# Two transformer layers with experts: expert numbers read once, stores on the queue of the engine that made them, and new ranks in the planner

## The chip, the cores and the metric

The kernel runs on one core of a Trainium2 chip, in one launch. The metric is the device time of one execution in microseconds (us). A core has five engines with an instruction queue each, worked off in order: TensorE (PE, matmuls and transposes), VectorE (DVE), ScalarE (ACT), GpSimd (POOL) and SyncE (SP), which computes nothing and issues DMAs. An instruction that waits holds up everything behind it in the queue of its engine. Semaphores tie the queues together.

## The reference

The input is 4,096 tokens of 128 numbers (16 sequences of 256). Two layers are applied; all is float32, and each half of a layer is followed by an addition and a layer norm:

```python
x = layernorm(x + attn0(rmsnorm(x)))   # 16 heads of 64, over the 256 tokens of a sequence
x = layernorm(x + shared(x) + experts0(x))   # best 2 of 8 experts, hidden 256, and a shared one
x = layernorm(x + attn1(x))            # a token's 16 heads of 8 attend to each other
x = layernorm(x + experts1(x))         # best 2 of 8 experts, hidden 512
```

An expert is GELU(x W1) W2, weighted by its softmax probability. The second attention is taken within each token: its scores are a 16 by 16 matrix per token.

## The kernel before

**Groups and waves.** Tokens are held in SBUF as eight groups of 512. Attention of layer 0 runs through the groups in units of two heads and one sequence: scores on TensorE (L574), row maxima on VectorE (L537), exponentials on ScalarE (L543), division by the sums on GpSimd (L558), transposes (L591) and the product with the values (L612) on TensorE. The expert halves run in waves over groups, `WAVES`: five waves in layer 0, three in layer 1 (the first holds groups 0 to 3, the second 4 and 5, the third 6 and half of 7). The other half of the last group goes through all experts densely (`sequence`, `dense`).

**One wave.** `route` computes on VectorE where each token goes (`r_pi`, L853) and which expert each tile of 128 rows has (`r_ei`, L867). `send` scatters the rows to DRAM on GpSimd, one indirect DMA per 128 tokens and choice (L905). `lists` then works through the tiles in fours, with these strands of its own:
- `loads_rows` loads four tiles of rows (L1014).
- `loads_first` loads per tile the weights of its expert. `expert_of` (L997) reads the expert's number from SBUF into a register of SyncE, and the DMA's address is worked out from that register. In layer 0 both weights come here (L1035, L1039), in layer 1 only the first one (L1039, 256 KB).
- `loads_second`, in layer 1 only, loads the second weight (L1048, 256 KB) into its own ring of buffers, and reads the expert's number again for it.
- `turns` transposes the rows (L1060), `firsts` multiplies by the first weights (L1098), `gelu` follows on ScalarE (L1071, L1077), `seconds` multiplies by the second weights (L1118).
- `stored` copies the result from PSUM into `yq` on VectorE or ScalarE (L270 or L272, in the helper `copied`) and stores four tiles to DRAM with one DMA (L1136), which SyncE issues.

When all tiles of a wave are stored, `gathered` fetches each token's two results on GpSimd (L934), and `normed` norms them: on VectorE (L399), or on ScalarE (L409) with two small GpSimd steps ahead. In layer 0 `attention1` follows for these tokens (L1216 to L1308), in layer 1 the output is stored (L1431 in `last`, L1595 in `sequence`) by SyncE. Only one wave at a time holds the buffers of `lists`.

**The order of the work.** Nothing of the order is left to a scheduler: the instructions are listed by a planner that runs while the kernel is built. Every strand is a generator that yields the time from which its next step can start and the engine it needs. `work` keeps a clock per engine from fixed costs, `moved` one for the DMA pipe. `everything` takes the strand with the best key: a time of favour and a rank from `KEYS` (for attention of layer 0 also `PACE`, one rank per half group), where a lower rank goes first among those that could start. `copied` gives a copy to the engine whose planned clock ends it first. So costs and ranks decide the listed order, the engine of a copy, and of a norm; what the chip then does can run ahead of or behind the plan, but each engine keeps its listed order.

```python
best = min(starts, key=lambda c: (max(c[0] - c[1].key[0], first), c[1].key[1:]))[1]
```

Of the kernel before, what the change touches and what calls it, by code (L numbers as in the profile page):

```python
# [28 lines left out]
LAST = NG - 1  # L29
# [8 lines left out]
def two_layers(  # L38
# [98 lines left out]
    def cleared(layer, w):  # L137
# [10 lines left out]

    INF = float("inf")
    KEYS = {  # L150
        "copy qk": (-0.126, 0.098),
        "copy v": (0.258, 0.464),
        "copy p": (0.365, 0.67),
        "copy o": (-2, 0.171),
        "softmax": (-0.332, 0.347),
        "softmax 2": (-0.557, 0.071),
        "summed": (-1.741, 0.444),
        "normalised": (0.126, 0.737),
        "heads": (-0.897, 0.036),
        "w route": (0.203, 0.017),  # L160
        "w send": (-0.299, 0.32),
        "w shared": (-0.925, 0.219),
        "w loads": (-0.335, 0.546),
        "w turns 0": (-0.74, 0.23),
        "w turns 1": (-0.883, 0.07),
        "w firsts 0": (-0.387, 0.019),
        "w firsts 1": (1.618, 0.545),
        "w gelu": (-0.526, 0.095),
        "w seconds 0": (-0.551, 0.301),
        "w seconds 1": (1.137, -0.645),  # L170
        "w stored": (-1.046, -0.735),
        "w gathered 0": (0.929, 0.295),
        "w gathered 1": (0.397, -0.379),
        "w qkv": (-1.874, 0.602),
        "w attention1": (0.552, 0.037),
        "w attention1 2": (0.862, 0.362),
        "w sums": (0.545, 0.099),
        "w normed": (-0.751, 0.178),
        "d loads": (-1.222, 0.561),
        "d route": (0.341, 0.516),  # L180
        "d firsts": (-0.612, -0.163),
        "d gelu": (0.532, 0.418),
        "d seconds": (-0.409, -0.744),
        "d added": (-0.448, 0.337),
        "d normed": (-0.4, 1.013),
    }
    PACE = [-1.37, 1.462, -1.273, -1.636, 1.503, -0.385, -0.54, 1.281]
    PACE += [1.979, 0.872, 0.936, -0.178, 0.47, 1.169, 0.679, 1.086]
    now = [0]
    COPY = -0.06  # L190
    SUMS = 7.789
    FAVOUR = 0.378
    SWITCH, SWITCH_BACK = 0.582, 1.515
    window, unit = [0, 0.0, 1.0], [P]
    clk = {"PE": 0.0, "DVE": 0.0, "ACT": 0.0, "POOL": 0.0, "SP": 0.0}
    table = ["exp"]
# [31 lines left out]
    def work(e, us, *after, ports=False, one=None, mode=P):  # L228

        at = max(clk[e], floor[0], *after)  # L230
        if ports and pool[0] - 0.15 > at:
            us += min(pool[0] - 0.15 - at, pool[1])
        clk[e] = (paced(at, us, mode) if e == "PE" else at + us) + SETUP[e]
        if one is not None:
            pool[:] = clk[e], one
        return clk[e] + 0.08

    def moved(size, *after, us=0.45, row=2048):

# [9 lines left out]
    def closed(place, at):  # L249
        ends[place[0]][place[1]] = at  # L250
        return at
# [129 lines left out]
        nc.gpsimd.tensor_tensor(r, v, mhalf[:, 0:n], ALU.pow)  # L381
        return r, work("POOL", 1.1, at)

    def normed(y, o, tag, at):
# [12 lines left out]
        if max(clk["DVE"], at) + 1.9 <= max(clk["ACT"], at) + 1.4:  # L397
            for c in range(n):
                nc.vector.tensor_scalar(  # L399
                    o[:, c, :], y[:, c, :], mv[:, c, 0:1], r[:, c : c + 1], ALU.subtract, ALU.mult  # L400
                )
            return work("DVE", 0.05 + 0.35 * n, at, ports=True)
# [7 lines left out]
        return work("ACT", 0.35 * n, at)  # L410

    def across(src, ring, at):

# [555 lines left out]
    def lists(r):  # L969
# [18 lines left out]
        starts = list(range(0, NT, QT))  # L988
        number = [min(NT, t0 + QT) - t0 for t0 in starts]
        N = len(starts)  # L990
        xqs, was, wbs, hs, xTs = {}, {}, {}, {}, {}
        gelued = {}
        downs = [0]
# [2 lines left out]
        def expert_of(t):  # L996
            return nc.values_load(  # L997
                r.expert[0:1, t : t + 1],
                engines=[mybir.EngineType.SP],
                min_val=0,  # L1000
                max_val=NE - 1,
                skip_runtime_bounds_check_because="the minimum with the last expert's number was taken",
            )
# [16 lines left out]
        def loads_first():  # L1020
            for i in range(N):
                if yields and i > 0 and urgent:
                    yield (lambda: INF if downs[0] < i else 0.0), None
                    held.remove("lists")
                    yield (lambda: INF if urgent or "lists" in held else 0.0), None
                    held.append("lists")
                for q in range(number[i]):

                    ring = WB if q % 2 and layer == 0 else WA
                    yield (lambda: max(r.listed, ring.free())), "SP"  # L1030
                    free = ring.free()
                    e = expert_of(starts[i] + q)
                    wa, k = ring.tile([P, 4, P], "wa")
                    if layer == 0:
                        nc.sync.dma_start(out=wa[:, 2:4], in_=second(e))  # L1035
# [3 lines left out]
                    nc.sync.dma_start(out=wa.rearrange("p c h -> p (c h)"), in_=w1[bass.ds(e * P, P), :])  # L1039
                    was[i, q] = wa, k, moved(131072 * (1 + layer), r.listed, free, us=0.45 + 0.4 * layer)  # L1040

        def loads_second():
            for i in range(N):
                for q in range(number[i]):
                    yield (lambda: INF if (i, q) not in was else WB.free()), "SP"
                    free = WB.free()
                    wb, k = WB.tile([P, 4, P], "wb")
                    nc.sync.dma_start(out=wb, in_=second(expert_of(starts[i] + q)))  # L1048
# [80 lines left out]
        def stored(i, place, po, at):  # L1129
            t0, n = starts[i], number[i]  # L1130
            yield (lambda: max(at, Y.free())), EITHER
            free = Y.free()
            y, k = Y.tile([P, QT, D], "yq")
            at = closed(place, copied(y[:, 0:n, :], po[:, 0:n, :], at, free))
            yield at, "SP"
            nc.sync.dma_start(  # L1136
                out=outs[layer][w][t0 * P : (t0 + n) * P, :].rearrange("(t p) d -> p t d", p=P),
                in_=y[:, 0:n, :],
            )
# [283 lines left out]
    def last(r, part):  # L1423
        g, c0, n = PARTS[part]
        at = yield from gathered(r, part, max(r.stored.values()))
        yield from taken("y1")
        y = sb.tile([P, n, D], FP, tag="y1", name="ye", bufs=1)
        at = yield from normed(tokens(part), y, "n1", at)
        yield at, "SP"
        b = c0 // 2  # L1430
        nc.sync.dma_start(  # L1431
            out=grouped(out, g)[:, b : b + n // 2], in_=y.rearrange("p (b c) d -> p b (c d)", b=n // 2)
        )
        held.remove("y1")
        return work("SP", 0.6, at)

    routed1 = []
    for i in range(len(WAVES[1])):
# [130 lines left out]
    def sequence(b=1):  # L1569
# [23 lines left out]
        at = yield from normed(x, y, "n1", at)  # L1593
        yield at, "SP"
        nc.sync.dma_start(out=grouped(out, LAST)[:, b], in_=y.rearrange("p c d -> p (c d)"))  # L1595
        held.remove("y1")
        work("SP", 0.6, at)

    begin(normalised(0), key("normalised"))
    begin(prepared(), key("normalised"))  # L1600
# [63 lines left out]
```

## Time and profile before

| what | us |
|---|---|
| median of 3 runs | 1215.32 (1213.84 to 1217.02) |
| the profiled execution, its own time | 1245.39 |
| its span, first to last instruction | 1243.7 |
| busy: TensorE (matmuls) | 1109.0 (89%) |
| busy: VectorE | 900.2 (72%) |
| busy: ScalarE | 706.0 (57%) |
| busy: GpSimd | 705.7 (57%) |
| granted TensorE clock, mean | 0.943 of full |
| DMA, mean over the span | 107 GB/s, 132.47 MB |

The profile shows one execution. Its times of single instructions, of stages and of waits add up to its own 1245.39 us and not to the median. A waiting line reads: engine and line, `<-` what ended the wait, then the sum of the waits in us, their number, the longest. A line of the timeline reads: start, length, engine, source line, operation, tiles, number; SPq is SyncE's queue of DMAs, and a merged line of several issues runs from the start of the first to the end of the last. A line of a source reads: operation, tiles, number, least/median/greatest duration in ns, first and last start.

### The profile page before, as it was taken

What the parts mean: (1) busy time and instruction counts of PE and PEld (TensorE: products, weight loads), DVE (VectorE), ACT (ScalarE), POOL (GpSimd) and SP (SyncE); (2) the same over time, 40 slices, a digit from 0 to 9 for tenths busy, and PEclk for the clock granted to TensorE, in tenths of its full rate; (3) what the DMA queues carried; (4) which work ended last, traced back from release to release, by engine and by line L of the source; (5) the groups of instructions that cost most, each with busy time, mean ns of one, the idle gap of its engine ahead of it and who ended that gap; (6) DMA issues with size and microseconds to landing.
All of it is one profiled execution on the core that took longest, in us unless ns stands there. A gap on an engine that the chain in (4) does not pass through costs nothing.

```text
span 1243.7 us, 22712 instructions
## 1 busy us (share of the span) xinstructions
PE 1109.0 (89%) x7336; PEld 814.5 (65%) x7336; DVE 900.2 (72%) x1811; ACT 706.0 (57%) x2050; POOL 705.7 (57%) x1089
## 2 busy tenths in 40 slices
PE   9999999979999999999998899987838896797883
PEld 5566667665665666766655677655738795697883
DVE  5767675478878888754877998888878795793433
ACT  5556566476665667676674687653544552342432
POOL 4434372557555468524769557767873546446666
PEclk9999999989999999999999999987888897798997
DMA  8900023430000021151003240135458874684952
GB/s 260 270 1 1 1 86 111 132 106 14 1 5 1 1 63 58 35 145 45 18 4 100 80 133 21 29 119 164 144 162 232 257 230 129 197 245 125 288 177 70
DMA packets 187208, 132.47 MB, mean 107 GB/s; under 512 B 12745, under 2 KB 171474, under 8 KB 187090
## 3 DMA queue, kind: packets, MB, share of 16 engines
q1 hardware_dynamic: 179410, 115.27, 31.6%
q0 software_dynamic: 7680, 15.74, 4.1%
q8 instruction: 59, 0.97, 0.3%
q14 instruction: 59, 0.48, 0.1%
HBM read 97.94 MB, written 33.03 MB: 105 GB/s over the span
## 4 chain that ended last, share of the span: by engine, by line
PE 66%; DVE 11%; POOL 8%; issue 6%; ACT 4%; DMA 2%; SPq 1%; ACTq 0%; DVEq 0%; POOLq 0%
PE s L574 9%; PE po L612 9%; PE t L591 9%; PE po_e L1118 6%; PE ph L1098 6%; POOL rows L905 5%; PE py L629 4%; PE pv L528 4%; PE pq L510 4%; PE pk L510 3%; DVE qk_prod L1216 2%; DMA xq<-rows 2%; PE po_d L1541 1%; POOL pr L558 1%; DVE sc L1220 1%
## 5 line engine op out<-in xcount | busy, mean ns | idle before, releaser
L558 POOL TENSOR_SCALAR pr<-pr,rs 128x256 f32<-128x256 f32 x512 | 253.0, 511 | 220.6 <-DVE rs L554 136.7
L543 ACT ACTIVATE pr<-s,nm 128x256 f32<-128x256 f32 x512 | 235.5, 474 | 26.1 <-DVE nm L537 23.0
L537 DVE TENSOR_REDUCE nm<-s 128x4 f32<-128x1024 f32 x128 | 156.1, 1220 | 58.0 <-PE s L574 53.2
L905 POOL DMA_INDIRECT rows<-x,r_pi x120 | 130.7, 1089 | 58.6 <-DVE r_pi L853 24.4
L934 POOL DMA_INDIRECT y<-outs,r_pi x120 | 120.0, 1000 | 65.8 <-issue 27.4
L612 PE MATMUL po<-pT,v 128*64 128x256 f32 x1024 | 146.0, 397 | 7.2 <-ACT h L1077 3.1
L1098 PE MATMUL ph<-xqT,wa 128*128 128x128 f32 x1028 | 132.8, 287 | 16.6 <-issue 14.2
L591 PE MATMUL t<-ident,pr 128*128 128x128 f32 x1024 | 144.4, 283 | 0.8 <-ACT h L1077 0.8
L591 PEld LDWEIGHTS t<-ident,pr 128*128 128x128 f32 x1024 | 115.7, 145 | 42.4 <-POOL pr L558 20.6
L1098 PEld LDWEIGHTS ph<-xqT,wa 128*128 128x128 f32 x1028 | 126.9, 202 | 22.6 <-issue 16.8
L270 DVE COPY pT<-t 128x512 f32<-128x512 f32 x163 | 106.8, 686 | 42.2 <-PE t L591 38.3
L574 PEld LDWEIGHTS s<-kT,qT 64*128 64x128 f32 x896 | 77.1, 186 | 84.2 <-issue 73.1
L574 PE MATMUL s<-kT,qT 64*128 64x256 f32 x896 | 127.0, 402 | 0.0
L1292 POOL TENSOR_TENSOR av_prod<-sc,qkv 128x1024 f32<-128x1024 f32 x35 | 89.9, 2577 | 50.7 <-ACT sc L1254 35.3
L272 ACT COPY oT<-po 128x256 f32<-128x256 f32 x99 | 36.9, 373 | 130.6 <-PE po L612 119.6
L612 PEld LDWEIGHTS po<-pT,v 128*64 128x64 f32 x1024 | 65.1, 137 | 67.6 <-issue 18.9
L543 ACT ACTIVATION_READ_ACCUMULATOR pr<-s,nm 128x1 f32 x512 | 105.5, 206 | 0.0
L1118 PE MATMUL po_e<-wb,h 128*128 128x128 f32 x648 | 84.3, 292 | 5.5 <-issue 5.5
L1118 PEld LDWEIGHTS po_e<-wb,h 128*128 128x128 f32 x648 | 82.6, 209 | 5.3 <-issue 4.8
L1216 DVE TENSOR_TENSOR qk_prod<-qkv 128x1024 f32<-128x1024 f32 x64 | 82.8, 1294 | 1.8 <-ACT qkv L272 1.8
L1267 DVE TENSOR_REDUCE o<-av_prod 128x64 f32<-128x1024 f32 x62 | 73.3, 1200 | 11.3 <-POOL apart L904 9.7
L1220 DVE TENSOR_REDUCE sc<-qk_prod 128x128 f32<-128x1024 f32 x64 | 78.1, 1220 | 2.2
(233 smaller groups left out, 1971.0 us busy)
## 6 DMA issues: line engine op xcount, KB each, us to landing
wa<-in_w_dram SPq DMA_DIRECT2D x190, 128.0 KB
wa<-in_w_dram SPq DMA_DIRECT2D x81, 256.0 KB
wb<-in_w_dram SPq DMA_DIRECT2D x81, 256.0 KB
xq<-rows SPq DMA_DIRECT2D x38, 256.0 KB
outs<-yq SPq DMA_DIRECT2D x38, 256.0 KB
rows<-clear SPq DMA_DIRECT2D x3, 1472.0 KB
rows<-clear SPq DMA_DIRECT2D x1, 2496.0 KB
rows<-clear SPq DMA_DIRECT2D x2, 1216.0 KB
```

The lines of the kernel that those rows point to most:

```text
L270: nc.vector.tensor_copy(o, i)
L537: nc.vector.tensor_reduce(nm[u], s, AX.X, ALU.max, negate=True)
L543: nc.scalar.activation(pr[u][:, i, :], s[:, i, :], AF.Exp, bias=nm[u][:, i : i + 1], accum_out=su[u][:, i : i + 1],)
L558: nc.gpsimd.tensor_scalar(pr[u][:, i, :], pr[u][:, i, :], rs[:, i : i + 1], 1.0, ALU.mult, ALU.mult)
L574: nc.tensor.matmul(sc[u][:, j, qc, :], q[part, ts(qc, P)], k[part, :], start=True, stop=True,)
L591: nc.tensor.transpose(t[:, kc, ts(qc, P)], pr[u][:, 2 * j + qc, ts(kc, P)], ident)
L612: nc.tensor.matmul(po[j * DH : (j + 1) * DH, :], vs[g, p // 4, 2 * b + kc][:, ts(h, DH)], pT[u][j][:, kc, :], start=(kc == 0), stop=(kc == 1),
L905: i = nc.gpsimd.indirect_dma_start(out=rows[layer][w][:, :], out_offset=bass.IndirectOffsetOnAxis(ap=r.pos[:, k, c : c + 1], axis=0), in_= ...
L934: nc.gpsimd.indirect_dma_start(out=y, out_offset=None, in_=outs[layer][w][:, :], in_offset=bass.IndirectOffsetOnAxis(ap=r.pos[:, k, c0 + c ...
L1098: nc.tensor.matmul(ph[:, q - q0, c, :], was[i, q][0][:, c, :], xTs[i][0][:, q, :], start=True, stop=True)
L1118: nc.tensor.matmul(po[:, q, :], hs[i, q][0][:, c, :], wbs[i, q][0][:, c, :], start=(c == 0), stop=(c == nh - 1))
L1216: nc.vector.tensor_tensor(m, q3[:, ts(j, HALF)].unsqueeze(2).to_broadcast(full), k3.unsqueeze(1).to_broadcast(full), ALU.mult)
```

## The change

Four things are changed.
- `loads_first` keeps the register value with the expert's number in `experts[i, q]`, and `loads_second` uses it and doesn't read the number again. The planner's cost of that step goes from 0.85 to 0.5 us.
- In `stored` the planner's clock tells which engine made the copy. A copy by ScalarE is followed at once by its store, issued by ScalarE (`nc.scalar.dma_start`); a copy by VectorE is stored by SyncE as before. `moved` takes the engine as an argument, and the cost of issuing a store is 0.55 us (it was 0.45).
- `normed` can tell which engine wrote its result, and the two stores of the output (`last`, `sequence`) leave from ScalarE where ScalarE wrote it.
- Of the ranks and times in `KEYS` and `PACE`, most are new, and so are `COPY`, `SUMS`, `SWITCH` and `SWITCH_BACK`. The other costs of the planner stay.

```diff
-        "copy qk": (-0.126, 0.098),
-        "copy v": (0.258, 0.464),
-        "copy p": (0.365, 0.67),
+        "copy qk": (-0.423, 0.098),
+        "copy v": (0.347, 0.324),
+        "copy p": (0.481, 0.679),
...
-        "w route": (0.203, 0.017),
-        "w send": (-0.299, 0.32),
+        "w route": (0.064, 0.017),
+        "w send": (-0.228, 0.393),
...
-    PACE = [-1.37, 1.462, -1.273, -1.636, 1.503, -0.385, -0.54, 1.281]
-    PACE += [1.979, 0.872, 0.936, -0.178, 0.47, 1.169, 0.679, 1.086]
+    PACE = [-1.67, 1.272, -1.466, -1.607, 1.408, -0.377, -1.53, 1.116]
+    PACE += [2, 1.308, 1.883, -0.142, 0.48, 2, 0.672, 1.559]
     now = [0]
-    COPY = -0.06
-    SUMS = 7.789
+    COPY = -0.142
+    SUMS = 7.454
     FAVOUR = 0.378
-    SWITCH, SWITCH_BACK = 0.582, 1.515
+    SWITCH, SWITCH_BACK = 1.195, 1.765
...
-    def moved(size, *after, us=0.45, row=2048):
+    def moved(size, *after, us=0.45, row=2048, e="SP"):
 
-        at = max(work("SP", us, *after) + 0.1, pipe[0])
+        at = max(work(e, us, *after) + 0.1, pipe[0])
...
-                    e = expert_of(starts[i] + q)
+                    e = experts[i, q] = expert_of(starts[i] + q)
...
-                    nc.sync.dma_start(out=wb, in_=second(expert_of(starts[i] + q)))
-                    wbs[i, q] = wb, k, moved(262144, free, us=0.85)
+                    nc.sync.dma_start(out=wb, in_=second(experts[i, q]))
+                    wbs[i, q] = wb, k, moved(262144, free, us=0.5)
...
+            was = clk["ACT"]
             at = closed(place, copied(y[:, 0:n, :], po[:, 0:n, :], at, free))
-            yield at, "SP"
-            nc.sync.dma_start(
+            by = "SP" if clk["ACT"] == was else "ACT"
+            if by == "SP":
+                yield at, "SP"
+            (nc.sync if by == "SP" else nc.scalar).dma_start(
                 out=outs[layer][w][t0 * P : (t0 + n) * P, :].rearrange("(t p) d -> p t d", p=P),
                 in_=y[:, 0:n, :],
             )
-            Y.done[k] = r.stored[i] = moved(n * 65536, at, row=512)
+            Y.done[k] = r.stored[i] = moved(n * 65536, at, us=0.55, row=512, e=by)
...
-        at = yield from normed(tokens(part), y, "n1", at)
-        yield at, "SP"
+        at, by = yield from normed(tokens(part), y, "n1", at, who=True)
+        if by == "DVE":
+            yield at, "SP"
         b = c0 // 2
-        nc.sync.dma_start(
+        (nc.scalar if by == "ACT" else nc.sync).dma_start(
```

More of the change, by code (lines that the diff above doesn't have):

```diff
@@ L150, in two_layers @@
     KEYS = {
-        "copy qk": (-0.126, 0.098),
-        "copy v": (0.258, 0.464),
-        "copy p": (0.365, 0.67),
-        "copy o": (-2, 0.171),
-        "softmax": (-0.332, 0.347),
-        "softmax 2": (-0.557, 0.071),
-        "summed": (-1.741, 0.444),
-        "normalised": (0.126, 0.737),
-        "heads": (-0.897, 0.036),
-        "w route": (0.203, 0.017),
-        "w send": (-0.299, 0.32),
-        "w shared": (-0.925, 0.219),
+        "copy qk": (-0.423, 0.098),
+        "copy v": (0.347, 0.324),
+        "copy p": (0.481, 0.679),
+        "copy o": (-0.737, 0.171),
+        "softmax": (-0.229, 0.347),
+        "softmax 2": (-0.557, 0.071),
+        "summed": (-1.761, 0.444),
+        "normalised": (-0.065, 0.737),
+        "heads": (0.327, 0.05),
+        "w route": (0.064, 0.017),
+        "w send": (-0.228, 0.393),
+        "w shared": (-0.692, 0.219),
         "w loads": (-0.335, 0.546),
-        "w turns 0": (-0.74, 0.23),
-        "w turns 1": (-0.883, 0.07),
+        "w turns 0": (-0.991, 0.23),
+        "w turns 1": (-0.064, 0.07),
         "w firsts 0": (-0.387, 0.019),
[L167 to L174, printed above, removed]
+        "w firsts 1": (1.892, 0.388),
+        "w gelu": (-0.878, 0.095),
+        "w seconds 0": (-0.618, 0.301),
+        "w seconds 1": (1.38, -0.546),
+        "w stored": (-1.103, -0.735),
+        "w gathered 0": (0.944, 0.213),
+        "w gathered 1": (0.549, -0.379),
+        "w qkv": (-1.726, 0.708),
         "w attention1": (0.552, 0.037),
@@ L177, in two_layers @@
         "w sums": (0.545, 0.099),
[L178 to L181, printed above, removed]
+        "w normed": (-0.936, 0.374),
+        "d loads": (-0.321, 0.447),
+        "d route": (0.462, 0.516),
+        "d firsts": (0.576, -0.087),
         "d gelu": (0.532, 0.418),
-        "d seconds": (-0.409, -0.744),
-        "d added": (-0.448, 0.337),
-        "d normed": (-0.4, 1.013),
-    }
-    PACE = [-1.37, 1.462, -1.273, -1.636, 1.503, -0.385, -0.54, 1.281]
-    PACE += [1.979, 0.872, 0.936, -0.178, 0.47, 1.169, 0.679, 1.086]
+        "d seconds": (-0.409, -0.8),
+        "d added": (-0.448, 0.609),
+        "d normed": (-0.866, 1.034),
+    }
+    PACE = [-1.67, 1.272, -1.466, -1.607, 1.408, -0.377, -1.53, 1.116]
+    PACE += [2, 1.308, 1.883, -0.142, 0.48, 2, 0.672, 1.559]
     now = [0]
-    COPY = -0.06
-    SUMS = 7.789
+    COPY = -0.142
+    SUMS = 7.454
     FAVOUR = 0.378
-    SWITCH, SWITCH_BACK = 0.582, 1.515
+    SWITCH, SWITCH_BACK = 1.195, 1.765
     window, unit = [0, 0.0, 1.0], [P]
@@ L382, in powered, with normed @@
         return r, work("POOL", 1.1, at)
-    def normed(y, o, tag, at):
+    def normed(y, o, tag, at, who=False):
         n = y.shape[1]
@@ L401, in normed @@
                 )
-            return work("DVE", 0.05 + 0.35 * n, at, ports=True)
+            at = work("DVE", 0.05 + 0.35 * n, at, ports=True)
+            return (at, "DVE") if who else at
         nb = sm.tile([P, n], FP, tag=f"{tag}_nb", name=f"{tag}_nb", bufs=1 if tag == "ln0" else 2)
@@ L409, in normed @@
             nc.scalar.activation(o[:, c, :], y[:, c, :], AF.Identity, bias=nb[:, c : c + 1], scale=r[:, c : c + 1])
-        return work("ACT", 0.35 * n, at)
+        at = work("ACT", 0.35 * n, at)
+        return (at, "ACT") if who else at
     def across(src, ring, at):
@@ L990, in lists @@
         N = len(starts)
+        experts = {}
         xqs, was, wbs, hs, xTs = {}, {}, {}, {}, {}
@@ L1434, in last @@
         held.remove("y1")
-        return work("SP", 0.6, at)
+        return work("SP" if by == "DVE" else "ACT", 0.6, at)
     routed1 = []
@@ L1592, in sequence @@
         y = sb.tile([P, 2, D], FP, tag="y1", name="ye", bufs=1)
-        at = yield from normed(x, y, "n1", at)
-        yield at, "SP"
-        nc.sync.dma_start(out=grouped(out, LAST)[:, b], in_=y.rearrange("p c d -> p (c d)"))
+        at, by = yield from normed(x, y, "n1", at, who=True)
+        if by == "DVE":
+            yield at, "SP"
+        (nc.scalar if by == "ACT" else nc.sync).dma_start(
+            out=grouped(out, LAST)[:, b], in_=y.rearrange("p c d -> p (c d)")
+        )
         held.remove("y1")
-        work("SP", 0.6, at)
+        work("SP" if by == "DVE" else "ACT", 0.6, at)
     begin(normalised(0), key("normalised"))
```

## The prediction

> **What bounds the kernel now.** I read the slices of the page first, then busy time by stage, then SyncE's own waits, then single lines.
>
> ```profile
> PE   9999999979999999999998899987838896797883
> ...
> PEclk9999999989999999999999999987888897798997
> DMA  8900023430000021151003240135458874684952
> ```
>
> One slice is 31.1 us. Up to slice 26 (some 800 us) TensorE is nearly full, at nearly full clock: this is attention of layer 0, and waves of experts run inside it. Behind that TensorE has holes, its clock drops, and the DMA engines are busy: this is layer 1. So the first 800 us have little to give, and the last 440 decide.
>
> ```profile
> 860.00:904.00 44.00, 33.96 (x209) 29.41 (x208) 38.29 (x69) 22.27 (x56) 31.00 (x44) 0.84 0.49 149
> 904.00:936.00 32.00, 11.77 (x74) 9.79 (x73) 23.31 (x27) 12.76 (x29) 22.71 (x28) 0.76 0.60 181
> 936.00:1030.00 94.00, 84.95 (x660) 80.55 (x658) 79.82 (x157) 47.79 (x83) 44.58 (x52) 0.92 0.81 241
> 1030.00:1041.00 11.00, 0.12 (x2) 0.10 (x1) 4.87 (x7) 0.48 (x1) 7.96 (x13) 0.65 0.33 108
> 1124.00:1138.00 14.00, 10.67 (x69) 10.32 (x68) 2.41 (x8) 3.43 (x8) 8.68 (x17) 0.76 0.23 71
> 1160.00:1197.00 37.00, 30.51 (x243) 29.23 (x242) 14.42 (x57) 13.64 (x28) 25.62 (x31) 0.96 0.91 265
> 1222.00:1243.70 21.70, 1.49 (x14) 1.30 (x12) 7.25 (x34) 4.48 (x11) 11.19 (x17) 0.64 0.21 61
> ```
>
> After the window come TensorE's busy time, weight loads, VectorE, ScalarE, GpSimd, granted clock, DMA share, GB/s. TensorE idles for 20.2 us of 904 to 936, 9.1 of 936 to 1030, 10.9 of 1030 to 1041, 6.5 of 1160 to 1197, and for 20.2 at the end, which is the last gathers, norms and stores.
>
> The changed parts sit in SyncE's queue:
>
> ```profile
> SPq L1035 <- PE po_e L1118: 95.4, 12, 33.7
> SPq L1136 <- ACT yq L272: 82.7, 10, 13.4
> ...
> SPq L1039 <- PE ph L1098: 21.7, 7, 10.8
> SPq L1048 <- PE po_e L1118: 14.5, 6, 4.6
> ...
> SPq L1136 <- DVE yq L270: 9.2, 3, 5.4
> ```
>
> ```profile
> L997 SPq TENSOR_LOAD <-r_ei x257: 3/270/1128, 168.1 to 1195.8; - x129
> L1136 SPq DMA_DIRECT2D outs<-yq x46: 359/448/1400, 211.4 to 1211.8; - x46
> L272 ACT COPY yq<-po_e x36: 478/585/672, 206.8 to 1205.3; 128x512 f32<-128x512 f32 x32, 128x384 f32<-128x384 f32 x4
> L270 DVE COPY yq<-po_e x10: 548/686/693, 201.6 to 1211.2; 128x512 f32<-128x512 f32 x6, 128x384 f32<-128x384 f32 x4
> ```
>
> A store at L1136 stands in SyncE's queue until its copy is made, and each load behind it waits too. ScalarE makes 36 of the 46 copies.
>
> **Own time against the median.** The profiled run took 1245.39 us (span 1243.70), the median is 1215.32, 30 us less. In 1026 to 1032 and 1139 to 1149 SyncE's single records, elsewhere a few tens of ns, come in steps of 0.7 us, and near there all engines stand still (1030 to 1041). I take such stretches for a burden of the profiled run, count no gain in them, and subtract what is left from the median.
>
> **Part 1, the register.** Layer 1 has 81 tiles (81 loads at L1048), each with two register loads at L997; the change drops one. That is 81 x (0.27 + some 0.045 us to the next record) = 25 us less on SyncE, from 927 to 1197; its address arithmetic (46 and 29 ns) and the DMA (373 ns) stay. Adding up SyncE's records there, it works 182 us and waits 88 of 270. Per tile that is 182/81 = 2.25 us, and TensorE needs (3.65 + 3.74)/4 = 1.85 us for a tile's 16 matmuls. So SyncE is the slower where neither waits, and 1.94 us without the load. But with a third of its time spent waiting it is not the bound throughout. The ends are 0 and TensorE's idle time in the stretches that loads feed, 9.1 + 6.5 = 15.6 us. In 1160 to 1197 the engines move 265 GB/s at a share of 0.91, so there the wire is next; in 936 to 1030 VectorE (79.8 of 94) is next. I take 3 us, a third of the 9.1.
>
> **Part 2, the stores.** 36 stores and, of the nine of the output, eight move to ScalarE if the choice of engine stays as it is. SyncE loses 44 x 0.45 = 20 us, ScalarE gains it. Behind a store on ScalarE stand exponentials and GELUs, and TensorE waits for the latter; but ScalarE works 127.7 of the 300 us from 900 to 1200, and TensorE's longest single wait for a GELU is 3.7 us. Ends 0 and 16 (36 x 0.45, were each on the path); I take 1 us lost.
>
> What the 82.7 us of waiting are worth, place by place. Five waits (13.5, 12.5, 12.7, 12.4, 3.0) lie before 800 us, where TensorE is full: nothing. At 902.6 and 911.4 (3.9, 8.4) the load behind needs scatters that end at 920: nothing. At 1042.8 and 1050.1 (7.7, 6.8) the weights of the next wave stand behind, but TensorE is then held by VectorE:
>
> ```profile
> PE t_x L419 <- DVE o L1308: 25.0, 3, 15.2
> ```
>
> One of these three runs to 1066.4; I take 1 us. At 1205.9 (4.8) nothing stands behind. The place that pays is the last wave:
>
> ```profile
> 1124.27 13.84 SPq L1136 DMA_DIRECT2D outs<-yq  x2
> 1138.79 13.64 SPq L1039 DMA_DIRECT2D wa<-in_w_dram  x9
> 1152.46 1.48 SPq L1014 DMA_DIRECT2D xq<-rows  x3
> ```
>
> Its expert numbers are there at 1121.2, yet SyncE stands at two stores until 1137.7, then issues nine weight loads, then the rows that TensorE waits for until 1157. The scatter of these rows ends at 1140.3, so some 1147 would do: 10 us. Of these the 0.7 us steps are 13.64 - 8 x 0.85 = 6.8 us (0.85 us apart in the same row at 1053.9), which I don't count; 3 us are left. The second of the two stores is VectorE's and stays on SyncE unless the plan gives that copy to ScalarE, hence 0 as the low end and 10 as the high one. I take 3. Part 2: 1 + 3 - 1 = 3 us gained.
>
> A rule speaks against part 2. The Trainium skill, DMA: Bandwidth & Descriptors, section Rules for kernel authors, holds that spreading DMAs over SP, ACT and GpSimd gives no bandwidth, because they share the same 16 engines, and saves only the sequencer's issue time. By the rule the stores are worth the 0.45 us of their issue, on an engine that waits a third of the time: 0, less 1 for ScalarE, so 1215.3 - 3 + 1 = 1213. By the row the worth lies in the standing ahead of the issue, which the rule doesn't count. I take the row, but only where something stands behind: 1209.
>
> **Part 3, the ranks and the planner's costs.** No row shows the new order. Its ends: the 20.2 us hole of 904 to 936 half filled (-10), or one more wait of the 15.2 us kind (+15). Larger PACE values in the late half groups let waves go ahead of attention at a tie, which brings the routing sooner and attention's end later. I take 0.
>
> Sum: 3 + 3 + 0 = 6 us, 1215.3 - 6 = 1209 us.
>
> **Rivals.**
> - *Hidden.* VectorE and GpSimd set the late stages: VectorE works 79.8 of 94 us in 936 to 1030, and the scatters before 921 and the gathers at the end are GpSimd's. SyncE's relief then becomes longer waiting at L1039 and L1048 for rings to come free (21.7 and 14.5 us now). 1215, between 1212 and 1219. Against it: the last wave's loads start visibly late.
> - *The turn of semaphores (slower).* By the trace's records SyncE's DMAs signal on eight semaphores in turn, and most (44 of the 46 stores) first wait for the DMA eight before to land. A store on ScalarE takes a turn too, where the program lists it, right at its copy. Then the SyncE load eight behind waits for copy, issue and landing (2.2 us idle, 4 to 6.7 under load). In the listed order of the program before, the load that would take the same turn went out at 931.2 and 951.6, and the copies ended at 934.3 and 955.0: with 0.45 and 4 us these loads would go 7.5 and 7.9 us later; over 13 stores of the late stage this makes some 42 us of standing. It decides once such a wait outlasts the seven DMAs in flight, about 7 x 0.9 = 6 us. If a third reaches TensorE: +14 - 6 = +8, 1223. Against it: only two waits pass 6 us. For ScalarE itself I find no such wait: each earlier holder of its turn had landed when the copy ended.
> - *The new order misplaces a step (slower).* In-order TensorE stands once more as at t_x: 15.2 - 6 = +9, 1224.
> - *The order also fills the hole at 904.* -6 - 10: 1199.
> - *The copies change engine.* If the new plan gives more copies to VectorE, fewer stores leave SyncE, and part 2 goes to 0: 1212, with the first rival.
>
> **How the numbers follow.** As forecast, 1204 to 1211.6: 0.40. Order helps as well, about 1199: 0.08. Hidden: 0.20. Turn of semaphores: 0.17. Misplaced step: 0.15. What this kernel's measurement can tell from no change is 0.3%, 3.6 us; so faster 0.48, same 0.20, slower 0.32. The range of 8 in 10 runs from 1197 to 1225, and the likeliest case's own from 1204 to 1211.6.
>
> **What would show it.** L997 has 176 loads, the time between two loads at L1048 falls by 0.3 us; L1136 stands mostly in ScalarE's queue; SyncE's wait for ScalarE's copies is gone and that at L1039 and L1048 grows; the first weight load of the last wave goes out within a few us of its expert numbers. TensorE's idle time between 936 and 1030 shrinks by a few us. The semaphore rival shows as SyncE waiting, ahead of a load, for a store's landing. I am wrong if attention ends over 5 us later, if the scatter of layer 1's first wave moves, or if VectorE keeps most copies.

## The result, and the profile after

The changed kernel takes 1224.68 us (median of 6 runs, 1220.5 to 1228.97) against 1215.74 for the kernel before (6 runs, 1213.84 to 1217.02): a ratio of 1.0072, 95% interval [1.0047, 1.0097]. It is 9 us slower where 6 us faster was forecast. The profiled execution after took 1220.5 us, span 1218.8.

The page's slices after, in the rows that the prediction showed of before (one slice is 30.5 us):

```profile
PE   9999999999999999979999959998776978589892
...
PEclk9999999999999999988999979999988989789897
...
DMA  8900023431000000213310303313667957778762
```

The shape is the old one: TensorE is full through attention, then come the holes of layer 1. New are the slices at 7 and 5 tenths from 518 and 701 us, both within attention.

The page of before took 1245.39 us and came from another chip than this one. The kernel before profiled once more, on a chip where it takes 1213.6 us, has a span of 1211.8 (experiment e1 below), and the traces of before and after are compared by that one. Its busy times by stage, then those of the changed kernel; a stage ends where the third wave's positions are known, where the fourth's are, with the last output projection of layer 0's attention, where the last wave of layer 1 is listed, and with the span. Columns: window, length, busy time of TensorE, weight loads, VectorE, ScalarE, GpSimd, granted clock, DMA share, GB/s.

```profile
0.00:450.80 450.80, 437.01 (x2754) 281.06 (x2754) 323.88 (x631) 280.20 (x942) 223.01 (x418) 0.98 0.24 68
450.80:650.70 199.90, 196.03 (x1287) 132.04 (x1287) 142.51 (x287) 136.75 (x427) 118.84 (x198) 0.99 0.19 57
650.70:846.20 195.50, 178.75 (x1175) 126.80 (x1174) 166.84 (x309) 125.94 (x365) 131.74 (x188) 0.97 0.27 78
846.20:1105.30 259.10, 208.75 (x1482) 191.73 (x1480) 221.81 (x404) 122.06 (x237) 148.84 (x182) 0.86 0.71 210
1105.30:1211.80 106.50, 81.46 (x644) 78.05 (x642) 44.40 (x186) 42.81 (x81) 77.21 (x105) 0.90 0.65 192
```

```profile
0.00:497.70 497.70, 491.77 (x3145) 314.70 (x3146) 366.13 (x709) 308.49 (x1056) 244.47 (x468) 1.00 0.21 62
497.70:678.10 180.40, 168.67 (x1065) 115.47 (x1065) 135.53 (x258) 108.53 (x331) 99.13 (x159) 0.95 0.21 63
678.10:860.70 182.60, 156.52 (x1009) 110.38 (x1006) 163.32 (x288) 107.97 (x309) 121.56 (x170) 0.93 0.28 84
860.70:1111.00 250.30, 194.50 (x1440) 176.69 (x1439) 220.67 (x424) 125.58 (x242) 157.59 (x190) 0.90 0.73 219
1111.00:1218.80 107.80, 79.09 (x623) 76.14 (x621) 41.35 (x175) 44.32 (x86) 76.90 (x105) 0.89 0.63 187
```

Read them as a sum. Attention ends at 860.7 instead of 846.2, **14.5 us later**, with the same matmuls done (some 5,217 in both). TensorE's idle time up to there is 450.8 - 437.01 and so on, 34.4 us in all, and 43.7 after: 9.3 more. The other 5 us are busy time: the clock is 1.00 up to 497.7, then only 0.95 and 0.93. Before had fallen to 0.97 at the lowest. From there to the last wave's list the changed kernel needs 250.3 us instead of 259.1 and **makes up 8.8**: TensorE is busy for 14 us less there. Its clock is 0.90 instead of 0.86, and the new plan gives no head sums to it (64 matmuls `o_sums`, two runs of 7.1 and 3.6 us in e1's chain, are gone; VectorE sums instead). Which of the two pays isn't shown. The last stage adds 1.3. So +14.5 - 8.8 + 1.3 = +7.0, which is the difference of the two spans.

**Where attention loses its time.** Within attention of e1 the longest wait of TensorE is 4.2 us. After has one of 12.4 us, from 701.9 to 714.3 (its row stands with e14 below). That is more than the 9.3 us of idle time that were added: all the other waits together are 3 us shorter than in e1. The low clock lies there too, and in a stretch of shorter waits from 515 on. Windows of after:

```profile
515.00:553.00 38.00, 30.16 (x147) 21.55 (x148) 31.30 (x34) 14.04 (x34) 23.56 (x33) 0.82 0.10 29
700.00:722.00 22.00, 9.60 (x35) 4.51 (x32) 21.79 (x21) 7.42 (x17) 16.90 (x22) 0.69 0.13 42
722.00:740.00 18.00, 18.00 (x130) 14.96 (x130) 17.67 (x25) 11.82 (x32) 7.73 (x8) 1.00 0.24 68
```

So this wait cost more than its own length: the two matmuls `pv` right behind it take 2.07 us, where the two at 525.9 took 1.02.

**What the mechanisms did.** They did what they say. There are 176 loads of an expert number (95 tiles in layer 0 and 81 in layer 1, one each), and 39 of the 46 stores leave from ScalarE (lines of the sources L1000 and L1142, after):

```profile
L1000 SPq TENSOR_LOAD <-r_ei x176: 262/272/1169, 168.2 to 1162.1; - x176
```

```profile
L1142 ACTq DMA_DIRECT2D outs<-yq x39: 366/367/431, 205.5 to 1188.7; - x39
...
L1142 SPq DMA_DIRECT2D outs<-yq x7: 359/371/571, 211.6 to 1172.9; - x7
```

SyncE's own waits, first e1 (kernel before), then after:

```profile
SPq L1136 <- ACT yq L272: 75.8, 13, 14.1
...
SPq L1039 <- PE ph L1098: 29.3, 14, 14.6
SPq L1136 <- DVE yq L270: 19.8, 4, 9.1
...
SPq L1048 <- PE po_e L1118: 11.2, 7, 4.1
```

```profile
SPq L1042 <- PE ph L1101: 48.7, 26, 7.7
...
SPq L1051 <- PE po_e L1121: 31.6, 33, 6.7
SPq L1142 <- DVE yq L270: 24.0, 3, 11.7
...
SPq L1051 <- DMA outs<-yq: 7.3, 3, 5.8
```

The 75.8 us of standing at ScalarE's copies are gone, and the waits for a free buffer of the weight rings (L1042, L1051) have gone from 40.5 us in 21 waits to 80.3 us in 59. SyncE reaches the next load sooner and waits there for TensorE to free its buffer. Order and mechanisms are both new in this comparison; e2 and e5 below part them. The semaphore rival's wait, for the landing of a store ahead of a load, is the last line: 7.3 us, where 42 had been worked out. In e5, which keeps the order that the 42 were worked out for, there are 11.1 us of it, in three rows of 4.1, 4.0 and 3.0.

### The profile page after: what moved, and what is told of

It reads as the page before. It is cut to its first block, busy times and chain, and to the rows that moved or that the text cites. A ratio compares the mean times of both kernels' runs of the same rounds, so it can differ in the third digit from the quotient of the medians.

```text
span 1218.8 us, 22385 instructions
## 1 busy us (share of the span) xinstructions
PE 1090.5 (89%) x7272; PEld 793.4 (65%) x7272; DVE 927.0 (76%) x1847; ACT 694.9 (57%) x2021; POOL 699.6 (57%) x1090
## 4 chain that ended last, share of the span: by engine, by line
PE 59%; POOL 15%; DVE 14%; issue 4%; ACT 4%; DMA 3%; SPq 0%; ACTq 0%; DVEq 0%; POOLq 0%
PE s L576 10%; PE po L614 9%; PE t L593 8%; POOL rows L907 7%; PE po_e L1121 5%; PE ph L1101 4%; PE pv L530 4%; PE pq L512 4%; PE py L631 4%; PE pk L512 3%; POOL pr L560 2%; DMA y<-outs,r_pi 2%; DVE o L1273 2%; POOL y L936 2%; POOL n_r L381 1%
## 5 line engine op out<-in xcount | busy, mean ns | idle before, releaser
L560 POOL TENSOR_SCALAR pr<-pr,rs 128x256 f32<-128x256 f32 x512 | 250.3, 506 | 233.4 <-DVE rs L556 157.9
L907 POOL DMA_INDIRECT rows<-x,r_pi x120 | 127.4, 1062 | 55.9 <-DVE r_pi L855 32.0
L593 PEld LDWEIGHTS t<-ident,pr 128*128 128x128 f32 x1024 | 112.6, 142 | 56.3 <-POOL pr L560 29.7
L614 PE MATMUL po<-pT,v 128*64 128x256 f32 x1024 | 143.2, 394 | 3.6 <-DVE pT L270 1.3
L1101 PE MATMUL ph<-xqT,wa 128*128 128x128 f32 x1028 | 128.3, 282 | 12.5 <-DVE xqT L270 6.5
L1101 PEld LDWEIGHTS ph<-xqT,wa 128*128 128x128 f32 x1028 | 122.7, 197 | 15.5 <-DVE xqT L270 6.9
L1298 POOL TENSOR_TENSOR av_prod<-sc,qkv 128x1024 f32<-128x1024 f32 x34 | 85.6, 2524 | 48.2 <-ACT sc L1260 26.7
L1222 DVE TENSOR_TENSOR qk_prod<-qkv 128x1024 f32<-128x1024 f32 x64 | 79.2, 1237 | 0.1
L530 PE MATMUL pv<-wv,hT 128*128 128x512 f32 x128 | 66.6, 605 | 12.9 <-ACT wT L272 12.4
L1121 PE MATMUL po_e<-wb,h 128*128 128x128 f32 x648 | 76.3, 276 | 0.0
```

What stands on the lines that cost most here:

```text
L530: nc.tensor.matmul(pv, hT[g][:, ts(c, P)], wv_s[:, ts(half, 512)], start=True, stop=True)
L560: nc.gpsimd.tensor_scalar(pr[u][:, i, :], pr[u][:, i, :], rs[:, i : i + 1], 1.0, ALU.mult, ALU.mult)
L593: nc.tensor.transpose(t[:, kc, ts(qc, P)], pr[u][:, 2 * j + qc, ts(kc, P)], ident)
L614: nc.tensor.matmul(po[j * DH : (j + 1) * DH, :], vs[g, p // 4, 2 * b + kc][:, ts(h, DH)], pT[u][j][:, kc, :], start=(kc == 0), stop=(kc == 1),
L907: i = nc.gpsimd.indirect_dma_start(out=rows[layer][w][:, :], out_offset=bass.IndirectOffsetOnAxis(ap=r.pos[:, k, c : c + 1], axis=0), in_= ...
L1101: nc.tensor.matmul(ph[:, q - q0, c, :], was[i, q][0][:, c, :], xTs[i][0][:, q, :], start=True, stop=True)
```

## The experiments

Chips differ for this kernel, and the experiments fell on five of them. On two, called prompt here, the kernel before takes 1213.6 us (43 and 19 runs); on three others, called late, 1245.6, 1249.2 and 1250.2 (11 runs each). Each ratio is against the kernel before on the same chip.

| run | chip | median us | ratio, 95% interval |
|---|---|---|---|
| e2 register alone, old order | prompt 1 | 1212.60 | 0.9987 [0.9977, 0.9998] |
| e5 both mechanisms, old order | prompt 1 | 1213.94 | 1.0008 [0.9994, 1.0022] |
| e7 new order, old mechanisms | prompt 1 | 1225.26 | 1.0093 [1.0065, 1.0120] |
| e18 changed kernel | prompt 2 | 1223.39 | 1.0094 [1.0068, 1.0121] |
| e19 as e5 | prompt 2 | 1214.26 | 1.0008 [0.9995, 1.0021] |
| e20 as e7 | prompt 2 | 1224.39 | 1.0105 [1.0079, 1.0131] |
| e16 both waits shortened | prompt 2 | 1229.49 | 1.0137 [1.0111, 1.0163] |
| e6 all old numbers | late 1 | 1322.93 | 1.0629 [1.0585, 1.0673] |
| e9 old COPY | late 1 | 1318.20 | 1.0589 [1.0542, 1.0636] |
| e10 old PACE | late 1 | 1370.50 | 1.0989 [1.0949, 1.1030] |
| e12 copies given back | late 1 | 1286.13 | 1.0332 [1.0288, 1.0376] |
| e13 changed kernel | late 2 | 1305.00 | 1.0442 [1.0400, 1.0484] |
| e14 subtraction on VectorE | late 2 | 1306.73 | 1.0472 [1.0431, 1.0512] |
| e15 ones on VectorE | late 2 | 1297.69 | 1.0385 [1.0342, 1.0428] |
| e17 late subtractions on VectorE | late 2 | 1302.96 | 1.0433 [1.0395, 1.0470] |
| e21 old attention, new rest | late 3 | 1286.20 | 1.0284 [1.0237, 1.0332] |
| e22 new attention, old rest | late 3 | 1318.71 | 1.0506 [1.0456, 1.0555] |

**Order or mechanisms: e1, e2, e5, e7.** e1 is the kernel before, for its trace. e2 keeps the number and nothing else. e5 has both mechanisms with the listed order of before on TensorE, VectorE, GpSimd and, stores aside, ScalarE. e7 is the reverse.

```diff
# e5, on the kernel before: the planner's account stays
+            was = clk["ACT"]
             at = closed(place, copied(y[:, 0:n, :], po[:, 0:n, :], at, free))
+            by = "SP" if clk["ACT"] == was else "ACT"
+            if by == "ACT":
+                store(nc.scalar)
             yield at, "SP"
+            if by == "SP":
+                store(nc.sync)
# e7, on the changed kernel: the account stays
-                    nc.sync.dma_start(out=wb, in_=second(experts[i, q]))
+                    nc.sync.dma_start(out=wb, in_=second(expert_of(starts[i] + q)))
-            (nc.sync if by == "SP" else nc.scalar).dma_start(
+            nc.sync.dma_start(
```

> The kernel before, profiled once more, to have a second trace of it: the profiled execution of the page took 1245.39 us where the plain runs took 1215.7. If the 0.7 us steps and the stand of all engines near 1030 and 1140 us were a burden of that one execution, this trace has a span of 1212 to 1218 us and lacks them, and the layer 1 stage is some 29 us shorter in it. If they belong to the kernel, the span is near 1244 again.

> The register part alone: layer 1 keeps the expert's number for the second weight, and the order of all other instructions stays as in the kernel before (the planner's cost of the step is left at 0.85). Theory of the order (the new ranks cost the time, the two mechanisms gain little): 1210 to 1215, at most 5 us faster. Theory that the mechanisms harm: it says nothing of this one, 1215 or slower.

> Both mechanisms in the order of the kernel before: numbers kept in the register, and stores of what ScalarE made issued by ScalarE right behind its copy; ranks, costs and the order on TensorE, VectorE and GpSimd as before. Theory of the order: 1206 to 1215, faster than or equal to before. Theory of the turn of semaphores (the mechanisms harm): 1219 to 1226, as slow as the changed kernel.

> The order of the changed kernel on TensorE, VectorE, GpSimd and ScalarE, with both mechanisms undone: numbers read twice, and SyncE issues every store at the place where the program lists it. Theory of the order: 1225 to 1240, slower than before, and by at least as much as the changed kernel. Theory that the mechanisms harm: 1212 to 1218, back at the time before.

The order alone costs 11.6 us, all that the change costs. In the old order the register is worth 1.0 us. The stores on top of it cost 1.3, which isn't clear of noise: the intervals of e2 and e5 overlap.

Where did the standing at ScalarE's copies go? SyncE's waits in e2, where the stores are still its own, then in e5:

```profile
SPq L1137 <- ACT yq L272: 76.9, 13, 15.0
...
SPq L1040 <- PE ph L1099: 33.0, 15, 16.1
...
SPq L1049 <- PE po_e L1119: 21.6, 15, 5.4
SPq L1137 <- DVE yq L270: 19.0, 4, 8.3
```

```profile
SPq L1142 <- DVE yq L270: 57.0, 4, 17.8
...
SPq L1042 <- PE ph L1101: 32.8, 12, 16.1
...
SPq L1051 <- PE po_e L1121: 21.6, 19, 4.4
```

The 76.9 us are gone, and the waits for the weight rings are as long as before (54.4 us for 54.6). Much of the standing has moved to the stores of VectorE's copies, which stay in SyncE's queue: 57.0 us for 19.0, in four waits each. The rest is spread over other waits of the queue. It was the register that lengthened the waits for the rings, from 40.5 us (e1) to 54.6.

Repeated on the second prompt chip the costs are the same:

> The changed kernel a third time, as the mark for the three beside it. If this chip is one on which the kernel before takes about 1214 us: 1.005 to 1.010 of it. If it is one on which the kernel before takes about 1247: 1.04 to 1.05 of it.

> The kernel before with both mechanisms of the change, the number read once and ScalarE's stores in ScalarE's queue, and the order of before on TensorE, VectorE, ScalarE and GpSimd: e5 again. On a chip where the kernel before takes about 1214 us: 1.000 as in e5. On a slow chip: if the order alone costs, within 0.5% of the kernel before; if stores in ScalarE's queue are held up there and hold up what ScalarE computes, 1.02 to 1.04.

> The order of the changed kernel on TensorE, VectorE, ScalarE and GpSimd, with the number read twice and every store in SyncE's queue: e7 again. On a chip where the kernel before takes about 1214 us: 1.009 as in e7. On a slow chip: if the order alone costs, 1.04 to 1.05 like the changed kernel beside it; if the stores in ScalarE's queue cost there, 1.01 to 1.02.

The traces show the cause at the same place. Attention's last matmuls in e5, then in e20:

```profile
L651 PE MATMUL py<-wout,oT x64: 275/275/377, 799.2 to 846.4; 128*128 128x128 f32 x64
```

```profile
L651 PE MATMUL py<-wout,oT x64: 275/275/377, 816.1 to 859.0; 128*128 128x128 f32 x64
```

On prompt chips attention ends between 844.1 and 846.7 us in all four traces of the old order (e1, e2, e5, e19), and between 859.3 and 868.7 in all five of the new one (after, e7, e16, e18, e20), with the mechanisms or without.

**Which of the new numbers: e6, e9, e10, e12.** The first theory on the order was VectorE's load: the lower `COPY` gives 39 copies more to it (391 for 352), and it is busy for 927 us instead of 899. e9 sets back `COPY`, e10 `PACE`, e6 all new numbers, each with the new account left in. e12 keeps order and account, and issues on ScalarE the 63 copies on which the two settings of `COPY` differ.

```diff
# e12
         if dve + COPY <= act:
-            nc.vector.tensor_copy(o, i)
+            if dve - 0.06 <= act:
+                nc.vector.tensor_copy(o, i)
+            else:
+                nc.scalar.copy(o, i)
             return work("DVE", us[0], *after)
```

> The changed kernel with all ranks, times and constants of the planner set back to the old ones; the two mechanisms and their new planner costs stay, so the order is a third one. Theory that the new numbers are at fault: 1211 to 1216. Theory that any order not fitted to the chip costs as much: 1220 to 1230, though no rank differs from before.

> The changed kernel with COPY alone back at -0.06 (VectorE is favoured less for copies: 359 of the 778 copies by VectorE where the changed kernel has 391 and the kernel before 352). Theory of VectorE's load (28 us more VectorE work in the changed kernel's trace set the late stages back): 1214 to 1219. Theory that the ranks delay attention of layer 0: 1221 to 1230.

> The changed kernel with PACE alone set back, the ranks of attention of layer 0 by half group (VectorE makes 422 copies then). Theory that yielding of attention in the late half groups costs the time: the last score matmul comes near 824 again (845 in the changed kernel) and the time is 1212 to 1218. Theory of VectorE's load: no gain, 1222 to 1232.

> The changed kernel, its order and its planner's account untouched, but 63 copies that go to VectorE only because COPY is -0.142 and not -0.06 are made by ScalarE (VectorE 328 copies, ScalarE 450). Theory of VectorE's load: VectorE's busy time falls by some 40 us and the time to 1212 to 1218. Theory that the order of TensorE is at fault: 1222 to 1230, no better, since ScalarE then holds back the exponentials.

These fell on a late chip; the changed kernel on another late chip has 1.0442 (e13). As far as ratios from two late chips can be compared, all three kernels with numbers set back are worse than that, by 1.4% (e9) to 5.2% (e10): each makes a third order, and none of the numbers can be judged alone. In e12 attention ends at 880.0, as in e13 (879.0), though VectorE has 35 us less to do (890.1 for 925.2): taking copies from it, which ScalarE then makes, doesn't bring attention forward. The theory of its load finds no support there. e12's ratio is lower than e13's all the same, behind attention, but it was taken on another chip.

**Waits of TensorE: e14, e15, e17, e16.** After has two long waits of TensorE that e1 has not. The first lies in attention; the second comes behind it, at 879. Here is the first as a chain, in rows of GpSimd, ScalarE and TensorE (after):

```profile
710.88 1.84 POOL L560 TENSOR_SCALAR pr<-pr,rs 128x256 f32<-128x256 f32 x4
712.70 0.61 POOL L1251 TENSOR_TENSOR sc<-sc,c_mx 128x256 f32<-128x256 f32 x1
```

```profile
713.34 0.42 ACT L1260 ACTIVATE sc<-sc 128x256 f32<-128x256 f32 x1 [7.27 <-POOL sc L1251]
713.66 0.56 ACT L272 COPY wT<-pw 9x512 f32<-9x512 f32 x1
```

```profile
714.27 2.07 PE L530 MATMUL pv<-wv,hT 128*128 128x512 f32 x2 [12.40 <-ACT wT L272]
```

A subtraction given to GpSimd stands behind scatters and softmax scalings; ScalarE's exponential waits for it, a copy stands behind the exponential, and TensorE waits for the place in PSUM that the copy frees. The second: TensorE's `pw` waits 11.1 us for a fill of ones, 0.13 us long, that stands behind 16 scatters. Theory M: such steps, misplaced by the new order, delay the end. Theory C: the end hangs on VectorE and GpSimd in the last waves, and the slack ahead absorbs them. e14 and e15 are to shorten one wait each, e16 both; e17 gives GpSimd's last four subtractions to VectorE.

```diff
# e14 (in e17: < 19 in place of != 7)
-            (nc.gpsimd if e == "POOL" else nc.vector).tensor_tensor(
+            (nc.gpsimd if e == "POOL" and (given.append(0) or len(given) != 7) else nc.vector).tensor_tensor(
                 sc1, sc1, mx.unsqueeze(2).to_broadcast(wide), ALU.subtract
# e15
-            nc.gpsimd.memset(r.w[:, :, NE:NE0], 1.0)
+            nc.vector.memset(r.w[:, :, NE:NE0], 1.0)
```

> The changed kernel itself, once more, as the mark for the three kernels beside it on the same chip. Both theories: 1.005 to 1.010 of the kernel before on the same chip (1.0072 at its first measurement).

> The changed kernel with one instruction given to another engine: the subtraction of the row maximum (line 1251) that in its trace starts on GpSimd at 712.70 us, behind the first-layer scatters and one block of softmax scalings, is issued on VectorE where it stands in the list; the account of times that lists everything is left alone, so every other instruction keeps its engine and its place. It should then start near 708.9, when VectorE has finished the reciprocal ahead of it, and TensorE's wait of 12.4 us before the matmul of the values at 714.3 should shrink to about 8.5. Theory M (the new order lost its time at TensorE's misplaced steps, and a step delayed in attention delays the end): 2 to 4 us less than the changed kernel. Theory C (the end is set by the chain of VectorE and GpSimd through the last waves of layer 1, 930 to 1110 us, and what attention loses is absorbed before it): within 1 us of the changed kernel.

> The changed kernel with the 0.13 us fill of ones for the dense expert's weights (line 1497) issued on VectorE where it stands in the list instead of GpSimd, whose queue in its trace lets it start only at 890.43 us, behind 16 scatters of tokens; nothing else moves. TensorE's transposition pw, which waited 11.1 us for it, should start near 880.5 and the wait shrink to about 1 us. Theory M: 3 to 8 us less than the changed kernel, since all of TensorE's queue behind it moves up. Theory C: within 1 us, since the first wave of layer 1 still waits for its scatters, which end at 923 in both.

> The changed kernel with the last four subtractions of the row maximum that it gives to GpSimd (line 1251, starts 1058, 1073, 1083 and 1092 us, 1.52 to 1.74 us each there, the last one behind a product of 2.3 us) issued on VectorE where they stand in the list (0.4 us each at the median there); nothing else moves. Theory M: within 1 us of the changed kernel, the steps that it names lie earlier. Theory C: positions of the last wave, known at 1108.7, come 2 to 4 us sooner, and the end with them: 2 to 4 us less. If the two engines take turns at one place in that stretch, a longer subtraction on VectorE (1.27 us is its longest) may eat half of it.

On the late chip e14 and e17 can't be told from the changed kernel, and e15 is 7 us below it, with intervals that overlap a little. e16 ran on a prompt chip:

> The changed kernel with both edits of e14 and e15: the subtraction at 712.70 us and the fill of ones at 890.43 us are issued on VectorE, all else keeps its engine and place. TensorE loses its waits before 714.3 (12.4 to about 8.5 us) and before 890.6 (11.1 to about 1). Theory M (a step of TensorE that the new order misplaced delays the end): 4 to 10 us less than the changed kernel beside it. Theory C (the end is set by the chain of VectorE and GpSimd in the last waves): within 2 us of it. On the chip of the last runs each edit alone gave within 8 us of the changed kernel, inside the scatter.

It takes 6 us *more* than e18 beside it, with intervals that overlap a little; there is no gain. The waits did shrink, but they aren't gone: `pw` waited 6.95 us where 1 was expected, and the first (row of TensorE in e16) 8.33:

```profile
714.75 2.08 PE L530 MATMUL pv<-wv,hT 128*128 128x512 f32 x2 [8.33 <-ACT wT L272]
```

So e16 asks what 4 us of each wait are worth, and not what the waits are worth. Set beside e18 record by record, TensorE is 3.7 us late at 547 (where the programs don't differ yet), 0.6 us early at 715, and 7.5 us late at 736. Half of this new loss is one wait that e18 hasn't, for VectorE's copy `v`:

```profile
726.34 0.48 PE L1190 MATMUL po<-b,wT 9*128 9x128 f32 x2 [3.62 <-DVE v L270]
```

VectorE had come to this place 3.4 us later than in e18, ahead of the edit (its product `qk_prod` starts at 706.45 and not 703.01), so TensorE was early only to wait for it. The other half falls where the clock is low. Clock and busy time of 720 to 740, in e16 and in e18:

```profile
720.00:740.00 20.00, 16.38 (x79) 13.14 (x79) 15.73 (x18) 9.95 (x25) 9.47 (x8) 0.73 0.01 3
```

```profile
720.00:740.00 20.00, 20.00 (x132) 15.41 (x132) 19.65 (x27) 13.20 (x34) 7.10 (x7) 0.96 0.18 53
```

Neither theory is settled by this. Theory M forecast a gain for shorter waits, and there is none; but 8.3 of the 12.4 us were never taken away. In e16 attention ends 6.9 us after e18's (868.7 and 861.8), and the span is 11.8 us longer. Traces of one and the same kernel differ as much: e7 ends attention at 866.9 with a span of 1230.3, e20 at 859.3 with 1221.1. So the lateness of e16 needn't be the edits' doing. In both pairs the later attention goes with the longer span. That speaks against theory C's slack, but doesn't test it.

**Cut at attention's end: e21, e22.** The ranks, paces and numbers are switched when attention has been listed, from old to new in e21 and from new to old in e22.

```diff
+        KEYS.update(LATER)
+        COPY, SUMS, SWITCH, SWITCH_BACK = -0.142, 7.454, 1.195, 1.765   # e21
         end["over"] = 0.0
```

> Both mechanisms; the old ranks, paces and numbers until attention is listed, the new ones from there on. All of TensorE's list up to attention's end is that of the kernel before. Theory S (each part's ranks do their own work: those of attention cost 14 us, those of the rest bring 9): attention ends at 846 as before, and the kernel takes 5 to 9 us less than the kernel before. Theory J (the ranks fit only the list that they were found with; the rest made up time because the end has slack against a late attention): attention ends at 846, and the kernel takes as long as the kernel before or longer.

> The reverse: the new ranks, paces and numbers until attention is listed, the old ones and the old account from there on. TensorE's list up to attention's end is that of the changed kernel. Theory S: attention ends at 861, and the rest takes its old 366 us from there: about 15 us more than the kernel before, 5 to 8 more than the changed one. Theory J: within 5 us of the changed kernel if the slack does it, or well above both if the old ranks don't fit this attention.

In e21 attention ends at 846.6, as in the kernel before, and yet it is 2.8% slower than that; e22 is 5.1% slower. Both needed 438 us from attention's end, where on late chips before needs 398 (its page) and the changed kernel 414 (e13). So theory S falls and J holds, on a late chip; e21 and e22 weren't run on a prompt one. Neither set of ranks is better in the rest by itself: each did best with the list that it was found with.

## Why the prediction was wrong

**Part 3 is the step that failed.** It put the new order at nothing for no other reason than that no row showed it ("No row shows the new order ... I take 0"). The runs put +11.6 us there (e7) and confirm it (e20, +10.8). In the traces this is TensorE in attention: it ends 14.5 us later, with one new wait of 12.4 us, which is more than all the idle time added, and 5 us of lower clock; 8.8 us are made up later. The prediction read the full TensorE of the first 800 us as "little to give". Where an engine is full there is little to win, but a new wait of it adds to the stage in full.

The rival *the new order misplaces a step*, 1224 us, forecast the sign, the size and the kind of event: TensorE stands once, for 12.4 us, because a step stands behind others in GpSimd's queue. The wait is in all five traces of the new order on prompt chips (8.3 to 12.4 us) and in none of the old. Its number is luck in part, since it left out both the lower clock and what is made up later. That this one wait carries through to the end stays open: no run takes it away, and shortening it by 4 us gave nothing. The prediction's own test, "wrong if attention ends over 5 us later", was the right one.

**Part 1** had the right mechanism and the wrong size: 1.0 us where 3 was taken (the interval goes from 0.2 to 2.8). A third of a stage's idle time was credited to SyncE without a wait of TensorE that showed it.

**Part 2** took 4 us of gain and 1 of loss. Measured on top of the register the sum is 1.3 us lost, not clear of 0; gain and loss weren't measured apart. The place that was to pay, the last wave, didn't. The prediction had named why: the second of the two stores is VectorE's and stays on SyncE, "hence 0 as the low end". SyncE in e1, in e5 and after:

```profile
1107.35 8.29 SPq L1136 DMA_DIRECT2D outs<-yq  x2
1116.18 7.82 SPq L1039 DMA_DIRECT2D wa<-in_w_dram  x9
1124.11 1.49 SPq L1014 DMA_DIRECT2D xq<-rows  x3
```

```profile
1115.21 0.37 SPq L1142 DMA_DIRECT2D outs<-yq  x1
1116.13 8.09 SPq L1042 DMA_DIRECT2D wa<-in_w_dram  x9
1124.30 1.48 SPq L1017 DMA_DIRECT2D xq<-rows  x3
```

```profile
1111.53 6.34 SPq L1042 DMA_DIRECT2D wa<-in_w_dram  x7
...
1129.05 1.64 SPq L1017 DMA_DIRECT2D xq<-rows  x3
```

In e1 SyncE starts on the weights 10.9 us after the wave is listed (1105.3). In e5 it has one store to wait for instead of two, and starts at the same time. After, it starts 0.5 us after the list (1111.0), as forecast, and that doesn't help either: the rows follow the last scatter, which GpSimd issues at 1124.2, by 4.9 us. In e1 they follow it (1119.7) by 4.4 us, just when SyncE is through with the weights. So on a prompt chip the 10 us of the page weren't there.

The *hidden* rival's mechanism, longer waits for the weight rings, shows where the register load goes in the old order (40.5 to 54.6 us), and where both mechanisms come to the new order (47.7 us in e20, 80.3 after). It isn't what became of the stores in the old order.

**The rule weighed in part 2.** The Trainium skill, DMA: Bandwidth & Descriptors, section Rules for kernel authors, grants a store on another queue only the issue time. For register and stores together it makes 2 us gained, and the row 6; measured in the old order is 0.3 us lost (e5). So the rule came nearer. The standing ahead of the issue, which it leaves out, was worth nothing here, because the queue then stood elsewhere, at VectorE's copies above all (57.0 us for 19.0).

**Own time against the median.** I took the 30 us as a burden of one execution. They belong to the chip: its eleven runs of the kernel before took 1241.0 to 1256.6 us. Places and waits read from that page, the last wave above all, were those of a late chip, and the time asked for was that of prompt ones.

## What to carry to other kernels

When a change comes with a newly found order, the order isn't a detail to be put at 0: a stage in which one engine is nearly full (TensorE was busy for 96% of attention before) can't get much faster, and every new wait of that engine in it adds up. Ask first where that stage ends in the new order. Every other order tried here was slower. A long wait of a queue is worth something only if the next thing in that queue could then go; look for what it will wait for instead. And a page whose own time is 2.5% off the median may come from another chip; read waits from a page that has the median's time.

## What the runs showed of the hardware

One program takes 1213.6 us on two chips and 1245.6 to 1250.2 on three; the changed one 1223.4 and 1305.0. Single instructions take equally long in both, but for TensorE's at a lower clock and for SyncE's records of register work in steps of 0.7 us (in the page of before and in e13, none in e1 or after). What differs most is when engines that wait for TensorE go on. On late chips the table of waits has rows whose releaser isn't found, "remote"; e13 has 98 us in 18 waits of such rows, and the changed kernel on a prompt chip none. The two longest of e13:

```profile
ACT h L1080 <- remote: 21.8, 1, 21.8
ACT h L1074 <- remote: 15.3, 6, 4.4
```

The first of them in the rows of TensorE and ScalarE (e13):

```profile
926.27 3.78 PE L1101 MATMUL ph<-xqT,wa 128*128 128x128 f32 x16 [5.50 <-DVE xqT L270]
...
947.24 2.08 PE L1101 MATMUL ph<-xqT,wa 128*128 128x128 f32 x8 [14.74 <-ACT h L1080]
```

```profile
946.05 1.14 ACT L1080 ACTIVATE h<-ph,r_bias 128x128 f32<-128x128 f32 x4 [21.78 <-remote]
```

The GELU `h` waits for nothing but these matmuls. On a prompt chip it starts 1.2 us after the first of them starts; here 19.8 us after, and TensorE then stands still for want of it. Set record by record against the same program on a prompt chip, over 30 steps of e13 that TensorE releases go on over 1 us late, up to 17.7, some 120 us added up. Nearly all lie within stretches in which GpSimd issues indirect DMAs or up to 3 us behind them, and these stretches are some 30% of the span. In the page of before it is over 20 steps, some 60 us, and they lie there too. That indirect DMAs hold up TensorE's signals on these chips is what this suggests, not what it shows: no kernel with fewer scatters was tried there.

The order matters here as well. Attention of the old order ends as early on late chips (845.8 in the page of before, 846.6 in e21) as on prompt ones. That of the changed kernel ends at 879.0 (e13) instead of 860.7. Why an order costs 1% on one kind of chip and 4% on the other stays open.
